# A graph layer on one core: the columns that VectorE and ScalarE pick are shared out anew

## The chip, the cores and the metric

The kernel runs on one core of one Trainium2 chip. The metric is the device time of one launch in microseconds, the median of several runs. The engines are TensorE (PE: matrix multiplies into PSUM), VectorE (DVE), ScalarE (ACT), GpSimd (POOL, which here issues indirect gathers) and SyncE (SP, which here issues other transfers).

## The reference

A message-passing layer over 412,500 edges between 12,500 nodes of 128 features, with a residual and a layer norm. The edges are sorted by their target node. Cut to what matters:

```
f0, f1 = x0 @ W1_0e, x1 @ W1_1o              # first half "feat", second half "self"
e0, e1 = feat0[src], feat1[src]              # a row of 128 per edge, gathered by its source
h  = gelu(gelu(edge_scalar @ W_mlp1) @ W_mlp2)
w00, w01, w10, w11 = h @ Wp_00, h @ Wp_01, h @ Wp_10, h @ Wp_11
mid0 = [w00*e0*ea0, w11*sum(e1*ea1)]         # products of weights, rows and edge attributes
mid1 = [(w01*e0)*ea1, w10*e1*ea0]
n0, n1 = segment_sum(mid0, dst), segment_sum(mid1, dst)
y  = cos*self + sin*(n @ W2)
out = layernorm(x + y)
```

## The kernel before

**Runs and chunks.** 512 edges are a run (`s`), four tiles of 128 edges (`q` = 0 to 3). Four runs are a chunk (`c`), and `k = s % 4` is a run's place in it. There are 806 runs. One loop over `s` writes out, by hand, the order of the instructions on TensorE, ScalarE, VectorE and SyncE; POOL's gathers run as buffers come free, up to 18 runs ahead (`LEAD = 19` buffers `G`).

**Start.** x is loaded, turned (`xT` keeps all of x in SBUF, features on partitions, one column per node), multiplied by the folded weights `wf`, and stored to a table in HBM.

**How a tile of rows gets into `G[s]`.** There are four ways.
- POOL gathers 128 rows of the table by an indirect transfer (line 210). This is the rule.
- In the first 18 runs it gathers rows of x instead. `turn_rows(s)` turns them (TensorE, then a copy by ScalarE), `features(s)` multiplies them by `wf` (TensorE, then a copy by ScalarE, line 569).
- In every 14th run from 36 on, SyncE fetches tile 3 row by row (`aid`, line 197): 16 rows at a time, 6 to 16 runs ahead.
- Tile 2 of some runs is picked by VectorE, and tile 1 of some by ScalarE. The engine loads the byte addresses of the sources' columns from a row in SBUF into its registers (`pick_nodes`, line 167), and copies each column of `xT` (128 partitions, one element each) into a tile `GT` (`pick`, lines 178 and 180). When 128 columns are there, `picked_rows` multiplies the tile by `wf` (TensorE, line 186) and ScalarE copies the result into `G` (line 187), two runs before its use.

`COLS = {DVE: 4, ACT: 5}` says that VectorE takes four runs for a tile and ScalarE five. VectorE loads two times 16 addresses a run, and copies 8 columns after its second multiply and 24 after its third. ScalarE loads 24 or 28 addresses a run. `COL_TURN` fixes at which `k` a finished tile is turned into rows: 0 for VectorE's tiles, 1 for ScalarE's.

**A run's work.** TensorE makes the weights (`weights`, line 550). VectorE multiplies weights and rows into `M` in three parts (`messages`: part 0 at line 592, parts 1 and 2 at line 596). TensorE sums `M` over the edges of each target with selection matrices (`segments`, lines 621 and 623), one run later. Each chunk, VectorE adds the sums to an accumulator (`add`, line 636), with a register load of up to four addresses at every fourth chunk (line 631), and makes the next selection (`select`, lines 577 and 585). For a later chunk ScalarE and TensorE compute the radial network (`radial`, `mlp1`, `mlp2`), all of whose PSUM tiles come from the two buffers called "h", as those of `picked_rows` and `moments` do.

**Norm.** When 512 nodes are complete (about every eighth chunk), `norm` at `k == 3` calls `moments`: TensorE multiplies (lines 653 and 656), ScalarE copies the result to `y` (line 661), VectorE takes mean and variance from PSUM (lines 665 and 666). At every second group `normalise` follows: VectorE, the square root on ScalarE (line 674), VectorE's reciprocal (line 675), scaling by ScalarE (line 688) and the store by SyncE (line 247).

At the loop's second run `addresses` scales the source numbers in SBUF into byte addresses (lines 152 and 154). `aid_load` brings them from HBM beforehand (lines 135 and 143).

Of the kernel before, what the change touches and what calls it, by code (L numbers as in the profile page):

```python
# [8 lines left out]
F32 = mybir.dt.float32  # L9
# [12 lines left out]
P = 128  # L22
# [25 lines left out]
AID_FROM = 36  # L48
AID_LEAD = 16
STEPS = 12  # L50
COLS = {DVE: 4, ACT: 5}
COL_Q = {DVE: Q - 2, ACT: Q - 3}
COL_TURN = {DVE: (8, 0), ACT: (16, 1)}
LNB = 2


# [1 line left out]
def gnn_kernel(ctx: ExitStack, tc: tile.TileContext, x, src, dst, ea4, ea8, w1_0, w1_1, wm1, wm2,  # L58
# [26 lines left out]
    def sub(ap, offset, dims):  # L85
        return bass.AP(tensor=ap.tensor, offset=ap.offset + offset, ap=dims)
# [24 lines left out]
    G, GT, Y = {}, {}, {}  # L111
    aided = range(AID_FROM, NS - 1, AID)

    picked = {}
    for e, per in COLS.items():
        picked[e], (t, k) = [], COL_TURN[e]
        while True:
            at = t + per + 1
            at += (k - at) % CH
            if at + 2 >= NS - 1:  # L120
                break
            picked[e].append((t, at, at + 2))
            t += per
    pick_of = {(e, s): i for e, g in picked.items() for i, (_, _, s) in enumerate(g)}
    assert AID_FROM >= raw_runs and AID_LEAD < LEAD and P % ROWS == 0 and STEPS <= AID
    assert all(raw_runs <= g[0][2] and 0 < len(g) <= 2 * P for g in picked.values())
    assert 0 < len(aided) <= P

    aid_at = cst.tile([len(aided), P], I32)
# [2 lines left out]
    def aid_load():  # L132


        nc.sync.dma_start(aid_at, sub(src, AID_FROM * SB + (Q - 1) * P, [[AID * SB, len(aided)], [1, P]]))
        for e, g in picked.items():
            cycle = CH // math.gcd(CH, COLS[e])
            for h in range(0, len(g), P):
                part = g[h:h + P]
                rows = cst.tile([len(part), P], I32, name=f"pick{len(pick_rows)}")  # L140
                for i in range(min(cycle, len(part))):
                    n = len(part[i::cycle])
                    nc.sync.dma_start(rows[i::cycle], sub(src, part[i][2] * SB + COL_Q[e] * P,
                                                          [[cycle * COLS[e] * SB, n], [1, P]]))
# [10 lines left out]

    picking = {e: [] for e in picked}

    def pick_nodes(e, s, part=0, parts=1):

        per = COLS[e]  # L160
        i, t = divmod(s - COL_TURN[e][0], per)
        if not 0 <= i < len(picked[e]):
            return
        if t == 0 and part == 0:
            GT[e, i] = wk.tile([P, P], F32, name=f"gt{list(picked).index(e)}", bufs=3)
        r0, r1 = (n * (P // 4) // (per * parts) * 4 for n in (t * parts + part, t * parts + part + 1))
        _, r = nc.values_load_multi_w_load_instructions(  # L167
            pick_rows[e, i][:, r0:r1], engines=[e], min_val=x_at, max_val=x_at + 4 * (N - 1),
            skip_runtime_bounds_check_because="addresses of columns")
        for k in range(r1 - r0):  # L170
            at = r[k].with_bounds(guaranteed_mod_val=0, out_of_modulus=4)
            picking[e].append((GT[e, i][:, r0 + k:r0 + k + 1], x_bytes[:, bass.ds(at, 4)].bitcast(F32)))

    def pick(e, n):

# [7 lines left out]
    def picked_rows(e, i):  # L183

        pt = ps.tile([P, P], F32, name="h")
        nc.tensor.matmul(pt, GT.pop((e, i)), wf, start=True, stop=True)  # L186
        nc.scalar.activation(G[picked[e][i][2]][:, COL_Q[e], :], pt, AF.Copy)  # L187

    def aid(s, t):

# [211 lines left out]
    def new_sums():  # L402
        A["next"] = wk.tile([P, 4, ACC], F32, name="acc")
# [237 lines left out]
    def moments(b, sums=None):  # L641
        n0, nn, full, tail, tiles = group(b)
        if not pend:
            Y["y"] = wk.tile([P, LNB, XB, P], F32, name="y", bufs=1)
            Y["v"] = wk.tile([P, LNB * XB, 2], F32, name="mv")
            nc.vector.memset(Y["v"], 1.0)
        j = len(pend)
        pend.append(b)
        pt = ps.tile([P, XB, P], F32, name="h")
        st = wk.tile([P, XB, 6], F32, name="bst")  # L650
        at = n0 - base[-1] if b in due[NCH - 1] else 0
        for t, k in tiles:
            nc.tensor.matmul(pt[:k, t, :], xT[:, n0 + t * P:n0 + t * P + k], ws, start=True, stop=sums is not None)
            if sums is None:
                for a in range(4):
                    nc.tensor.matmul(pt[:k, t, :], A["now"][:, a, at + t * P:at + t * P + k], wpost[:, a, :],  # L656
                                     start=False, stop=a == 3)
            else:
                nc.vector.tensor_tensor(pt[:k, t, :], pt[:k, t, :], sums[:k, t, :], op=OP.add)
        if full:  # L660
            nc.scalar.activation(Y["y"][:, j, :full, :], pt[:, :full, :], AF.Copy)  # L661
        if tail:
            nc.scalar.activation(Y["y"][:tail, j, full, :], pt[:tail, full, :], AF.Copy)
        for t, k in tiles:
            nc.vector.bn_stats(st[:k, t, :], pt[:k, t, :])  # L665
            nc.vector.bn_aggr(Y["v"][:k, j * XB + t, :], st[:k, t, :])

    def normalise(last=False):
        y, mv = Y["y"], Y["v"]
        n = len(pend) * XB  # L670
        a = wk.tile([P, 4, LNB * XB], F32, name="rs")
        v, r, u, m = a[:, 0, :n], a[:, 1, :n], a[:, 2, :n], a[:, 3, :n]
        nc.vector.tensor_scalar(v, mv[:, :n, 1], EPS, None, op0=OP.add)
        nc.scalar.activation(u, v, AF.Sqrt)
        nc.vector.reciprocal(r, u)

        nc.vector.tensor_tensor(u, r, r, op=OP.mult)
        nc.vector.scalar_tensor_tensor(u, v, -0.5, u, op0=OP.mult, op1=OP.mult)
        nc.vector.scalar_tensor_tensor(r, u, 1.5, r, op0=OP.add, op1=OP.mult)
        nc.vector.scalar_tensor_tensor(m, mv[:, :n, 0], -1.0, r, op0=OP.mult, op1=OP.mult)  # L680
        for j, b in enumerate(pend):
            for t, k in group(b)[4]:
                i = j * XB + t
                if last and t % 2:
                    nc.vector.tensor_scalar(y[:k, j, t, :], y[:k, j, t, :], r[:k, i:i + 1], m[:k, i:i + 1],
                                            op0=OP.mult, op1=OP.add)
                    continue
                nc.scalar.activation(y[:k, j, t, :], y[:k, j, t, :], AF.Identity,
                                     bias=m[:k, i:i + 1], scale=r[:k, i:i + 1])
            store_nodes(nc.sync, out, b, y[:, j])  # L690
        pend.clear()

    def norm(bs, last=False):
        for b in bs:
            moments(b)
            if not last:
                move_sums()
                new_sums()
            if len(pend) == LNB or b == 0:
                normalise(last)  # L700
        if last and pend:
            normalise(last)

    odd_f = cst.tile([1, 1], F32)
    odd_i = cst.tile([1, 1], I32)
# [9 lines left out]
    def general():  # L715
# [96 lines left out]
                                         out_offset=bass.IndirectOffsetOnAxis(ap=to, axis=0))  # L812
        for b in range(NG):
            moments(b, load_nodes(b, sums))
            if len(pend) == LNB:
                normalise()
        if pend:
# [2 lines left out]
    with tc.manual_schedule(engines={PE, ACT, DVE, SP}):  # L820
# [41 lines left out]
            mlp2(1)  # L862
        weights(0, range(Q))
        select(0)
        turn_rows(0)
        features(0)
        A["now"] = A["next"]
        clearing = []
        pick_nodes(ACT, 0)
        for s in range(NCH * CH + CH):  # L870
            c, k = divmod(s, CH)
            if s + LEAD - 1 < NS:
# [37 lines left out]
            pick_nodes(ACT, s + 1)  # L910
            if s + 1 < raw_runs:
                turn_rows(s + 1)
            if s < NS:
                messages(s, 0)
                messages(s, 1)
                pick_nodes(DVE, s, 0, 2)
                pick(DVE, P // 16)
                messages(s, 2)
                pick_nodes(DVE, s, 1, 2)
                pick(DVE, P)  # L920
            if s + 1 < raw_runs:
                features(s + 1)
# [47 lines left out]
```

## Time and profile before

| | |
|---|---|
| Median of 3 runs | 3773.7 us (3766.81 to 3779.11) |
| Profiled execution | 3772.84 us, span 3771.0 us |
| Mean granted TensorE clock | 0.914 |
| PE busy | 3274.6 us (87%) |
| DVE busy | 3106.1 us (82%) |
| POOL busy | 2682.6 us (71%) |
| ACT busy | 2594.3 us (69%) |
| Transfers | 240.07 MB, mean 64 GB/s |

The span runs from the first to the last instruction of one profiled execution. Busy time counts an engine's instructions on data. Register loads, semaphores and the issuing of transfers are not in it. "Idle before" a group of instructions is the time in which the engine did nothing just ahead of them; behind the arrow stands what ended it, and "issue" where the profile shows no other engine or transfer. A name such as DVEq is the instruction queue of that engine.

### The profile page before, as it was taken

What the parts mean: (1) busy time and instruction counts of PE and PEld (TensorE: products, weight loads), DVE (VectorE), ACT (ScalarE), POOL (GpSimd) and SP (SyncE); (2) the same over time, 40 slices, a digit from 0 to 9 for tenths busy, and PEclk for the clock granted to TensorE, in tenths of its full rate; (3) what the DMA queues carried; (4) which work ended last, traced back from release to release, by engine and by line L of the source; (5) the groups of instructions that cost most, each with busy time, mean ns of one, the idle gap of its engine ahead of it and who ended that gap; (6) DMA issues with size and microseconds to landing.
All of it is one profiled execution on the core that took longest, in us unless ns stands there. A gap on an engine that the chain in (4) does not pass through costs nothing.

```text
span 3771.0 us, 139554 instructions
## 1 busy us (share of the span) xinstructions
PE 3274.6 (87%) x28566; PEld 2859.2 (76%) x28566; DVE 3106.1 (82%) x28801; ACT 2594.3 (69%) x21604; POOL 2682.6 (71%) x2821
## 2 busy tenths in 40 slices
PE   5888898888898889888889898898898888888998
PEld 4677777777777778777778777777787777777877
DVE  3488888888888888888888888888888888888886
ACT  2367677777767767767777677776776677767774
POOL 7567777777777777777777777777777777767770
PEclk8999898998988999899998899999899999989889
DMA  8222222323222223222223222222322222222220
GB/s 203 47 51 67 61 56 65 64 57 70 61 58 64 63 57 68 64 55 62 62 63 67 61 63 61 61 62 61 68 62 59 59 64 61 60 63 63 58 61 15
DMA packets 579462, 240.07 MB, mean 64 GB/s; under 512 B 483793, under 2 KB 528744, under 8 KB 578616
## 3 DMA queue, kind: packets, MB, share of 16 engines
q0 software_dynamic: 90080, 184.66, 19.1%
q1 hardware_dynamic: 467766, 39.95, 8.7%
q10 hardware_dynamic: 20770, 6.47, 0.7%
q8 instruction: 252, 4.13, 0.5%
q14 instruction: 594, 4.87, 0.4%
HBM read 218.04 MB, written 12.80 MB: 61 GB/s over the span
## 4 chain that ended last, share of the span: by engine, by line
DVE 51%; issue 12%; PE 10%; SPq 9%; DVEq 6%; ACT 5%; DMA 4%; POOL 2%; ACTq 0%; POOLq 0%
DVE gt L178 29%; DVE M L596 14%; SPq L197 7%; DVEq L167 6%; DVE M L592 3%; ACT gt L180 3%; PE sums L621 2%; POOL G L210 2%; PE sums L623 2%; SPq L193 2%; PE h L656 2%; DMA G<-table,idx 1%; DVE acc L636 1%; PE w L550 1%; PE h L517 1%
## 5 line engine op out<-in xcount | busy, mean ns | idle before, releaser
L210 POOL DMA_INDIRECT G<-table,idx x2743 | 2613.7, 953 | 981.2 <-issue 758.4
L180 ACT ACTIVATE gt<-xT 128x1 f32 x19968 | 1953.4, 189 | 255.9 <-issue 254.2
L178 DVE COPY gt<-xT 128x1 f32 x25216 | 1680.1, 144 | 374.2 <-issue 362.4
L623 PE MATMUL sums<-own,M 128*128 128x96 f32 x6446 | 1342.7, 292 | 63.2 <-DVE M L596 62.7
L621 PE MATMUL sums<-own,M 128*128 128x96 f32 x6446 | 1374.7, 297 | 25.0 <-DVE M L596 24.8
L621 PEld LDWEIGHTS sums<-own,M 128*128 128x128 f32 x6446 | 1063.9, 205 | 115.4 <-DVE M L596 31.1
L623 PEld LDWEIGHTS sums<-own,M 128*128 128x128 f32 x6446 | 1061.4, 207 | 84.1 <-DVE M L596 83.2
L550 PE MATMUL w<-wpb,h 64*128 64x128 f32 x6448 | 726.8, 310 | 255.8 <-DVE M L596 254.9
L550 PEld LDWEIGHTS w<-wpb,h 64*128 64x128 f32 x6448 | 540.4, 200 | 426.8 <-DVE M L596 305.8
L596 DVE TENSOR_TENSOR M<-w,G 128x384 f32<-128x384 f32 x1576 | 861.2, 547 | 0.1
L521 ACT ACTIVATE h<-h 128x512 f32<-128x512 f32 x404 | 216.2, 585 | 225.0 <-PE h L517 219.2
L592 DVE TENSOR_TENSOR M<-w,G 128x256 f32<-128x256 f32 x788 | 321.6, 408 | 3.6 <-ACT G L187 2.0
L517 PE MATMUL h<-eT,w1b 64*128 64x128 f32 x3232 | 299.9, 339 | 4.2 <-ACT eT L510 4.2
L517 PEld LDWEIGHTS h<-eT,w1b 64*128 64x128 f32 x3232 | 255.8, 237 | 29.6 <-issue 12.5
L187 ACT ACTIVATE G<-h 128x128 f32<-128x128 f32 x353 | 96.2, 272 | 261.1 <-PE h L186 218.1
L532 PE MATMUL h<-h,w2b 64*64 64x256 f32 x3232 | 236.5, 392 | 7.4 <-ACT h L521 6.3
L537 ACT ACTIVATE h<-h 128x512 f32<-128x512 f32 x404 | 213.6, 578 | 25.1 <-PE h L532 20.0
L532 PEld LDWEIGHTS h<-h,w2b 64*64 64x64 f32 x3232 | 111.1, 133 | 60.5 <-ACT h L521 16.1
L186 PE MATMUL h<-wf,gt 128*128 128x128 f32 x706 | 145.7, 289 | 4.1 <-ACT eT L510 4.1
L585 DVE TENSOR_TENSOR own<-oh,e 128x512 f32<-128x512 f32 x202 | 139.7, 692 | 7.1
L665 DVE BATCH_NORM_STATS2 bst<-h 128x6 f32<-128x128 f32 x98 | 26.9, 274 | 131.2 <-ACT y L661 123.0
L510 ACT ACTIVATE eT<-h 128x128 f32<-128x128 f32 x202 | 53.8, 267 | 111.1 <-PE h L508 105.2
(112 smaller groups left out, 1364.5 us busy)
## 6 DMA issues: line engine op xcount, KB each, us to landing
G<-table SPq DMA_DIRECT2D x7040, 0.5 KB
G<-table,idx POOLq DMA_INDIRECT x2743
e<-in_edge_attr SPq DMA_DIRECT2D x201, 64.0 KB
xt<-in_x SPq DMA_DIRECT2D x24, 256.0 KB
table<-ft ACTq DMA_DIRECT2D x24, 256.0 KB
xt<-in_edge_attr SPq DMA_DIRECT2D x24, 256.0 KB
out<-y SPq DMA_DIRECT2D x24, 256.0 KB
xt<-in_dst SPq DMA_DIRECT2D x5, 256.0 KB
```

What stands on the lines that cost most here:

```text
L167: _, r = nc.values_load_multi_w_load_instructions(pick_rows[e, i][:, r0:r1], engines=[e], min_val=x_at, max_val=x_at + 4 * (N - 1), skip_r ...
L178: nc.vector.tensor_copy(to, col)
L180: nc.scalar.activation(to, col, AF.Copy)
L197: nc.sync.dma_start(G[s][r0 + k:r0 + k + 1, Q - 1, :].bitcast(U8), table_bytes[bass.ds(r[k], P * 4)].rearrange("(a k) -> a k", a=1))
L210: nc.gpsimd.indirect_dma_start(out=G[s][:, q, :], out_offset=None, in_=x if s < raw_runs else table, in_offset=bass.IndirectOffsetOnAxis(a ...
L517: nc.tensor.matmul(p1[h][:, j // 2, j % 2, :], w1b[rows, j, :], eT[c][rows, :], start=True, stop=True)
L532: nc.tensor.matmul(p2[r][k * HID:(k + 1) * HID, h * n:(h + 1) * n], w2b[rows, :], H1[c][h][rows, k * n:(k + 1) * n], start=True, stop=True)
L550: nc.tensor.matmul(WP[i][:, q, :], H2[c][q % 2][rows, k, q // 2, :], wpb[rows, :], start=True, stop=True)
L592: nc.vector.tensor_tensor(M[s][:, :, :, :MUL], w[:, :, :2 * MUL].rearrange("p q (a u) -> p q a u", a=2), g[:, :, None, :MUL].to_broadcast( ...
L596: nc.vector.tensor_tensor(M[s][:, :, j, MUL:].rearrange("p q (i u) -> p q i u", i=3), w[:, :, None, (2 + j) * MUL:(3 + j) * MUL].to_broadc ...
L621: nc.tensor.matmul(flat[:, bass.ds(at, 4 * FIRST_HALF)].bitcast(F32), M[s][:, q, 0, :], own[:, 3 * WIDE:], start=False, stop=False)
L623: nc.tensor.matmul(sb[:, 1:, bass.ds(at, 4 * WIDE)].bitcast(F32), M[s][:, q, 1, :], own[:, :3 * WIDE].rearrange("p (a j) -> p a j", a=3), ...
```

## The change

- VectorE picks 36 columns a run instead of 32, ScalarE 28 instead of about 25.6. VectorE loads 8, 12 and 16 addresses, each followed by as many copies, after its first, second and third multiply. Columns are counted through, so that a tile may end within a group; the load is then split in two. Over the whole run VectorE fills 222 tiles instead of 197, ScalarE 171 instead of 156, and POOL issues 2703 gathers from the table instead of 2743.
- A picked tile is turned into rows two runs after its last column, at whatever `k` that falls.
- The addresses come by 32 transfers instead of 10.
- `statistics` is split from `moments`. It reads `y` in SBUF instead of PSUM, and it and `normalise` come one run later, at `k == 0`, behind that run's multiplies and copies; in the last chunk they follow at once.
- `turn_rows` and `features` run two runs ahead instead of one; those of the first two runs stand ahead of the loop.

```
-COLS = {DVE: 4, ACT: 5}
+SLOTS = {DVE: [(8, 12, 16)], ACT: [(28,)]}
-COL_TURN = {DVE: (8, 0), ACT: (16, 1)}
+COL_FROM = {DVE: 11, ACT: 16}
...
+    slot_at = {}
+    for e, cycle in SLOTS.items():
+        slot_at[e], n = {}, 0
+        for s in range(COL_FROM[e], NS):
+            for slot, k in enumerate(cycle[(s - COL_FROM[e]) % len(cycle)]):
+                slot_at[e][s, slot] = (n, n + k)
+                n += k
...
+            last = P * (len(picked[e]) + 1)
+            at = next((s for (s, _), (_, z) in slot_at[e].items() if z >= last), NS) + 2
             if at + 2 >= NS - 1:
                 break
-            picked[e].append((t, at, at + 2))
+            picked[e].append(at + 2)
...
+    def pick_nodes(e, s, slot):
+        a, z = slot_at[e].get((s, slot), (0, 0))
+        z = min(z, P * len(picked[e]))
+        while a < z:
+            i, r0 = divmod(a, P)
+            r1 = min(P, r0 + z - a)
+            if r0 == 0:
+                GT[e, i] = wk.tile([P, P], F32, name=f"gt{list(picked).index(e)}", bufs=3)
+            _, r = nc.values_load_multi_w_load_instructions(
+                pick_rows[e, i][:, r0:r1], engines=[e], ...)
...
+            a += r1 - r0
...
-        for t, k in tiles:
-            nc.vector.bn_stats(st[:k, t, :], pt[:k, t, :])
+
+    def statistics(b):
+        j = pend.index(b)
+        st = wk.tile([P, XB, 6], F32, name="bst")
+        for t, k in group(b)[4]:
+            nc.vector.bn_stats(st[:k, t, :], Y["y"][:k, j, t, :])
             nc.vector.bn_aggr(Y["v"][:k, j * XB + t, :], st[:k, t, :])
...
-        turn_rows(0)
-        features(0)
+        for s in range(min(2, raw_runs)):
+            turn_rows(s)
+            features(s)
...
-            if s + 1 < raw_runs:
-                turn_rows(s + 1)
+            if s + 2 < raw_runs:
+                turn_rows(s + 2)
             if s < NS:
-                messages(s, 0)
-                messages(s, 1)
-                pick_nodes(DVE, s, 0, 2)
-                pick(DVE, P // 16)
-                messages(s, 2)
-                pick_nodes(DVE, s, 1, 2)
-                pick(DVE, P)
-            if s + 1 < raw_runs:
-                features(s + 1)
+                for part in range(3):
+                    messages(s, part)
+                    pick_nodes(DVE, s, part)
+                    pick(DVE, P)
+            if s + 2 < raw_runs:
+                features(s + 2)
...
-            if k == (1 if end else 3) and 0 < c <= NCH:
-                norm(due.get(c - 1, []), last=c == NCH)
+            if k == 0 and c > 1:
+                norm_on(due.get(c - 2, []))
+            if c == NCH and k == 1:
+                norm_last(due[c - 1])
+            if k == (1 if end else 3) and 0 < c < NCH:
+                norm(due.get(c - 1, []))
```

More of the change, by code (lines that the diff above doesn't have):

```diff
@@ L112, in gnn_kernel @@
     aided = range(AID_FROM, NS - 1, AID)
+    slot_at = {}
[5 more added lines that the diff above has]
+                n += k
     picked = {}
-    for e, per in COLS.items():
-        picked[e], (t, k) = [], COL_TURN[e]
+    for e in SLOTS:
+        picked[e] = []
         while True:
-            at = t + per + 1
-            at += (k - at) % CH
+            last = P * (len(picked[e]) + 1)
+            at = next((s for (s, _), (_, z) in slot_at[e].items() if z >= last), NS) + 2
             if at + 2 >= NS - 1:
                 break
-            picked[e].append((t, at, at + 2))
-            t += per
-    pick_of = {(e, s): i for e, g in picked.items() for i, (_, _, s) in enumerate(g)}
+            picked[e].append(at + 2)
+    pick_of = {(e, s): i for e, g in picked.items() for i, s in enumerate(g)}
     assert AID_FROM >= raw_runs and AID_LEAD < LEAD and P % ROWS == 0 and STEPS <= AID
-    assert all(raw_runs <= g[0][2] and 0 < len(g) <= 2 * P for g in picked.values())
+    assert all(raw_runs <= g[0] and 0 < len(g) <= 3 * P for g in picked.values())
     assert 0 < len(aided) <= P
@@ L136, in aid_load @@
         for e, g in picked.items():
-            cycle = CH // math.gcd(CH, COLS[e])
+            n = sum(sum(run) for run in SLOTS[e])
+            cycle, ahead = n // math.gcd(n, P), P // math.gcd(n, P) * len(SLOTS[e])
+            assert all(z - a == ahead for a, z in zip(g, g[cycle:]))
             for h in range(0, len(g), P):
@@ L141, in aid_load @@
                 for i in range(min(cycle, len(part))):
-                    n = len(part[i::cycle])
-                    nc.sync.dma_start(rows[i::cycle], sub(src, part[i][2] * SB + COL_Q[e] * P,
-                                                          [[cycle * COLS[e] * SB, n], [1, P]]))
+                    k = len(part[i::cycle])
+                    nc.sync.dma_start(rows[i::cycle], sub(src, part[i] * SB + COL_Q[e] * P,
+                                                          [[ahead * SB, k], [1, P]]))
                 pick_tiles.append(rows)
@@ L156, in gnn_kernel @@
     picking = {e: [] for e in picked}
[L158 to L172, printed above, removed]
+    def pick_nodes(e, s, slot):
[7 more added lines that the diff above has]
+            _, r = nc.values_load_multi_w_load_instructions(
+                pick_rows[e, i][:, r0:r1], engines=[e], min_val=x_at, max_val=x_at + 4 * (N - 1),
+                skip_runtime_bounds_check_because="addresses of columns")
+            for k in range(r1 - r0):
+                at = r[k].with_bounds(guaranteed_mod_val=0, out_of_modulus=4)
+                picking[e].append((GT[e, i][:, r0 + k:r0 + k + 1], x_bytes[:, bass.ds(at, 4)].bitcast(F32)))
+            a += r1 - r0
     def pick(e, n):
@@ L186, in picked_rows @@
         nc.tensor.matmul(pt, GT.pop((e, i)), wf, start=True, stop=True)
-        nc.scalar.activation(G[picked[e][i][2]][:, COL_Q[e], :], pt, AF.Copy)
+        nc.scalar.activation(G[picked[e][i]][:, COL_Q[e], :], pt, AF.Copy)
     def aid(s, t):
@@ L649, in moments @@
         pt = ps.tile([P, XB, P], F32, name="h")
-        st = wk.tile([P, XB, 6], F32, name="bst")
         at = n0 - base[-1] if b in due[NCH - 1] else 0
@@ L691, in normalise, with norm, norm_on, norm_last @@
         pend.clear()
-    def norm(bs, last=False):
+    def norm(bs):
         for b in bs:
             moments(b)
-            if not last:
-                move_sums()
-                new_sums()
-            if len(pend) == LNB or b == 0:
-                normalise(last)
-        if last and pend:
-            normalise(last)
+            move_sums()
+            new_sums()
+    def norm_on(bs):
+        for b in bs:
+            statistics(b)
+            if len(pend) == LNB or b == 0:
+                normalise()
+    def norm_last(bs):
+        for b in bs:
+            moments(b)
+            statistics(b)
+            if len(pend) == LNB:
+                normalise(True)
+        if pend:
+            normalise(True)
     odd_f = cst.tile([1, 1], F32)
@@ L814, in general @@
             moments(b, load_nodes(b, sums))
+            statistics(b)
             if len(pend) == LNB:
@@ L864, in gnn_kernel @@
         select(0)
-        turn_rows(0)
-        features(0)
+        for s in range(min(2, raw_runs)):
+            turn_rows(s)
+            features(s)
         A["now"] = A["next"]
         clearing = []
-        pick_nodes(ACT, 0)
+        pick_nodes(ACT, 0, 0)
         for s in range(NCH * CH + CH):
@@ L909, in gnn_kernel @@
             pick(ACT, P)
-            pick_nodes(ACT, s + 1)
-            if s + 1 < raw_runs:
-                turn_rows(s + 1)
+            pick_nodes(ACT, s + 1, 0)
+            if s + 2 < raw_runs:
+                turn_rows(s + 2)
             if s < NS:
-                messages(s, 0)
-                messages(s, 1)
-                pick_nodes(DVE, s, 0, 2)
-                pick(DVE, P // 16)
-                messages(s, 2)
-                pick_nodes(DVE, s, 1, 2)
-                pick(DVE, P)
-            if s + 1 < raw_runs:
-                features(s + 1)
+                for part in range(3):
[4 more added lines that the diff above has]
+                features(s + 2)
             if k == (1 if end else 2) and 0 < c <= NCH:
                 add(c - 1)
-            if k == (1 if end else 3) and 0 < c <= NCH:
-                norm(due.get(c - 1, []), last=c == NCH)
+            if k == 0 and c > 1:
[4 more added lines that the diff above has]
+                norm(due.get(c - 1, []))
                 clearing += [(c, a) for a in range(4)] if c - 1 in due and c < NCH else []
```

## The prediction, made before the changed kernel was run

> **What bounds the kernel now.** I read the busy times and the whole-core groups first, then the stretch of steady work, then the waits, then single instructions. One step of the main loop is one run of 512 edges. The engines' busy times, and the groups of VectorE (DVE), of the gathering engine (POOL) and of ScalarE (ACT), each with count | busy us, mean ns | idle before it:
>
> ```profile
> span 3771.0 us, 139554 instructions
> ...
> PE 3274.6 (87%) x28566; PEld 2859.2 (76%) x28566; DVE 3106.1 (82%) x28801; ACT 2594.3 (69%) x21604; POOL 2682.6 (71%) x2821
> ...
> L178 DVE COPY gt<-xT 128x1 f32 x25216 | 1680.1, 144 | 374.2 <-issue 362.4
> L592 DVE TENSOR_TENSOR M<-w,G 128x256 f32<-128x256 f32 x788 | 321.6, 408 | 3.6 <-ACT G L187 2.0
> L665 DVE BATCH_NORM_STATS2 bst<-h 128x6 f32<-128x128 f32 x98 | 26.9, 274 | 131.2 <-ACT y L661 123.0
> L210 POOL DMA_INDIRECT G<-table,idx x2743 | 2613.7, 953 | 981.2 <-issue 758.4
> L180 ACT ACTIVATE gt<-xT 128x1 f32 x19968 | 1953.4, 189 | 255.9 <-issue 254.2
> ```
>
> The steady stretch from 500 to 3500 us, with each engine's busy time, and VectorE's idle time within the same stretch by what ended it:
>
> ```profile
> core 0: us, PE busy (x) PEld busy (x) DVE busy (x) ACT busy (x) POOL busy (x), PEclk, DMA share, GB/s
> 500.00:3500.00 3000.00, 2635.40 (x23124) 2301.98 (x23124) 2557.87 (x24145) 2159.79 (x18336) 2206.11 (x2315) 0.92 0.29 62
> DVE gt L178 <- issue: 305.1, 765, 1.3
> DVE bst L665 <- ACT y L661: 92.6, 19, 7.5
> ```
>
> VectorE looks only 85% busy (2557.87 of 3000). But 305.1 us more are idle before the column copies of line 178 with no partner to wait for ("issue"), and 92.6 us before the statistics. Together that is 2955.6 us of 3000, 98.5%. It almost never waits for data: the multiplies of line 592, which need both TensorE's weights and the gathered rows, have 3.6 us of idle in the whole run. VectorE is the bound, and its "issue" idle belongs to its own instruction stream.
>
> What that idle is: before each group of column copies the addresses are loaded into registers. The two kinds of register loads on VectorE's queue, then one step of VectorE, then the chain of waits over the same stretch:
>
> ```profile
> L167 DVEq TENSOR_LOAD <-pick x1576: 1093/1122/1740, 149.6 to 3716.9; - x197
> L631 DVEq TENSOR_LOAD <-first_at x51: 342/348/766, 135.8 to 3751.0; - x51
> 2024.96 0.42 DVE L592 TENSOR_TENSOR M<-w,G 128x256 f32<-128x256 f32 x1
> 2025.29 0.55 DVE L596 TENSOR_TENSOR M<-w,G 128x384 f32<-128x384 f32 x1
> 2025.81 0.58 DVE L178 COPY gt<-xT 128x1 f32 x8
> 2026.30 0.55 DVE L596 TENSOR_TENSOR M<-w,G 128x384 f32<-128x384 f32 x1
> 2027.27 1.54 DVE L178 COPY gt<-xT 128x1 f32 x24 [0.42 <-issue]
> 2028.73 0.41 DVE L592 TENSOR_TENSOR M<-w,G 128x256 f32<-128x256 f32 x1
> ...
> 2026.20 0.06 DVEq L167
> 2026.26 0.12 DVE gt L178 x2
> 2026.38 0.47 DVE M L596
> 2026.85 0.42 issue
> ```
>
> A load of 16 addresses takes 1122 ns, one of 4 (line 631 loads four at once) 348 ns: (1122 − 348)/12 = 64.5 ns an address and 90 ns fixed. So 8 cost 0.61 us and 12 cost 0.86 us (estimates from these two rows). A copy costs 61 ns (24 of them between 2027.27 and 2028.73), so **the load of an address costs as much as the copy it serves**. It is free only as far as VectorE still has issued work to run. Here it has not: the second load begins at about 2026.17 (1.10 us ahead of the copies at 2027.27; the chain turns to it at 2026.20). The work issued before it ends at 2026.76: the multiply from 2026.30 with 0.46, what such a multiply holds the engine when work follows it at once (the chain has 0.47). Cover 0.59 us, uncovered 0.51. The first load, behind 24 copies and two multiplies, leaves 0.06 (2025.29 + 0.46 to 2025.81). Uncovered now: 0.57 us a step.
>
> Second in line is POOL. Its gathers follow one another every 1.25 us:
>
> ```profile
> 2027.42 0.94 POOL L210 DMA_INDIRECT G<-table,idx  x1 [0.31 <-issue]
> 2028.66 0.94 POOL L210 DMA_INDIRECT G<-table,idx  x1 [0.30 <-issue]
> POOL G L210 <- DVE M L596: 134.8, 129, 9.9
> POOL G L210 <- PE h L559: 31.1, 16, 3.5
> ```
>
> 2743 × 1.25 = 3429 us: nearly full as well. But it is POOL that waits 134.8 us for VectorE to free row buffers, and not the reverse.
>
> **The change, part by part.** All is set against the profiled execution: 3772.84 us, span 3771.0, 0.9 us under the median of 3773.7. A measurement of this kernel tells about 0.3% (11 us) from no change.
>
> *More columns on VectorE.* The new order of instructions has 222 tiles of 128 columns where there were 197: 25 × 128 = 3200 copies more, at 61 ns = **+195 us**, all on the bound. Nothing hides them.
>
> *Three groups in place of two.* A step becomes: 256-wide multiply, load 8, copy 8; 384-wide multiply, load 12, copy 12; 384-wide multiply, load 16, copy 16. It has 790 such steps. Uncovered load time by the step shown above: instructions are issued every 0.04 us (9 in the 0.36 from 2025.81 to 2026.17). The 12-load stands where the second load stood, behind 8 copies and a multiply: 1.10 − 4 × 0.0645 = 0.84 less cover 0.59 = 0.25. The 16-load starts 13 × 0.04 = 0.52 after the first of 12 copies that last 0.73; cover 0.73 − 0.52 + 0.46 = 0.67, uncovered 0.43. The 8-load (0.58) stands behind 16 copies and the 256-wide multiply (0.33, 2024.96 to 2025.29): 17 × 0.04 = 0.68 of 0.97, cover 0.62, nothing uncovered; I keep 0.06, since the first load of today shows that much. Together 0.74 against 0.57: 0.17 × 790 = **+134 us**. Bounds: all covered, −0.57 × 790 = −450; only the one multiply covers, 0.25 + 0.38 + 0.64 = 1.27, +553. I take the value by the quoted step, as the same engine, instructions and loads are in it.
>
> *Tiles that end within a group.* 128 is no multiple of the groups, so 146 loads are split: 146 × 0.09 = **+13 us** (0 if covered).
>
> *Statistics a step later.* Now VectorE, right after TensorE's products for 512 nodes have been asked for, waits for ScalarE's copy out of them, 131.2 us in all; 128 of it lie before the last group, 23 waits of 5.3 us on average. Afterwards a whole step of VectorE's own work (4.5 us: 3000 us hold 666 steps by the 256-wide multiplies) comes first, and the input is the copy in SBUF. Left over: 23 × 0.8 = 18. What is late next is the square root:
>
> ```profile
> L592 DVE TENSOR_TENSOR M<-w,G 128x256 f32<-128x256 f32 x666 | 271.8, 408 | 1.2 <-DMA G<-table 0.2 <-PE h L186 0.2 <-PE h L508 0.2
> DVE rs L675 <- ACT rs L674: 6.6, 13, 0.6
> SPq L247 <- ACT y L688: 217.7, 23, 21.4
> ACT G L187 <- PE h L186: 218.1, 122, 3.1
> ```
>
> The reciprocal waits 0.5 us for it today, because ScalarE has then just written y and stands idle; a step later ScalarE may have 14 columns ahead of it (14 × 0.098 = 1.4 us, 12 times; +17 at most of this kind, +64 if the whole 5.3 us came back). I take +5. Sum 128 − 18 − 5 = **−105 us** (bounds −128 and −46). The output stores move with it on SyncE's queue, where they already hold 217.7 us; behind them stand the single-row transfers of the fourth tile, issued six steps or more ahead (over 27 us). Cost 0; if that cover were gone, up to one 21.4 us stall each.
>
> *Input-gathered rows two steps ahead.*
>
> ```profile
> DVE M L592 <- ACT ft L569: 57.3, 18, 14.3
> 100.00:130.00 30.00, 24.79 (x209) 21.10 (x209) 11.70 (x55) 8.80 (x17) 19.03 (x21) 0.94 0.17 43
> L143 SPq DMA_DIRECT2D pick<-in_src x10: 309/592/787, 82.4 to 88.4; - x10
> 107.98 0.24 DVE L152 TENSOR_SCALAR aid_at<-aid_at 55x128 int32<-55x128 int32 x1
> ```
>
> In the first 18 steps VectorE waits 57.3 us for ScalarE's rows; the first 14.3 comes ahead of the loop and stays. Of the other 43 TensorE, busy 24.79 of 30 us there, can give back no more than its idle sixth of some 110 us: **−20 us** (bounds 0 and −43). SyncE must issue 32 address transfers instead of 10 (22 × 0.59 = 13 us) before VectorE scales them in the loop's second step; today they are out at 89 and wanted at 108. Cost 0, at most +13.
>
> *ScalarE* gets 171 − 156 = 15 tiles more, 1920 copies × 0.098 = 188 us, hidden in its 1177 us of idle time; *POOL* loses 40 gathers, −50 us, off the bound. Cost 0 both. If ScalarE's cover were gone, 188.
>
> Sum: 195 + 134 + 13 − 105 − 20 = +217; 3772.8 + 217 = **3990 us**.
>
> **The rivals.** *Loads hidden (faster).* If the issuing runs ahead so fast that a load begins with its group's predecessor, cover is the whole predecessor and the next multiply: 0.95 for the 12-load, 1.19 for the 16-load, and nothing stays uncovered. VectorE would then need 3772.8 + 195 − 450 + 13 − 105 − 20 = 3406, and POOL ends last: 3771 − 134.8 − 31.1 − 50 = 3555, some 3600 with its own late starts. It decides as soon as the uncovered time falls under 0.57 − (195 + 13 − 125)/790 = 0.46 us a step. Against it: today's second load has the same predecessor as the new 12-load and is not hidden. [...]
>
> *Loads no worse than now.* The three gaps together stay at 0.57 us: 195 + 13 − 105 − 20 = +83, 3856 us. For it speaks only that the loads are smaller; the longest, 16, keeps its length.
>
> *ScalarE's and TensorE's turn-taking.* Picked tiles are now turned to rows at any step of a chunk, also where the radial network needs the same two PSUM buffers. If half of 393 tiles made TensorE wait 1.8 us (218.1/122 is what ScalarE waits for such a tile), 353 us would join TensorE's 3274.6 busy and 496 idle: 4124 at worst. It decides from 122 tiles on (219 us); against it: TensorE has that idle time and gets more as VectorE slows.
>
> That the change does not do what it says is not open: the order of instructions has the 3200 copies and the 40 gathers fewer.
>
> **How the numbers follow.** The forecast gets 0.76, equal loads 0.10, turn-taking 0.05, hidden loads 0.09. The range goes from the equal loads, 3850, to the forecast with 0.12 us a step more uncovered (95 us), 4085. Faster than the bound 0.09, within it 0.02, slower 0.89.
>
> **What would show it.** Right: VectorE's column copies 28416, their idle time from 374 to about 500 to 560 us with idle before groups of 12 and of 16; the statistics' wait from 131 to some 20; POOL's wait for VectorE up to several hundred us; 4.8 us a step. Wrong: idle before the column copies under 300 us, POOL without waits, or TensorE and ScalarE waiting for each other at line 186's tiles while VectorE waits at its multiplies.

## The result, and the profile after

The changed kernel took 4117.8 us (median of 4 runs, 4108.6 to 4120.5) against 3774.7 before: ratio 1.090, 95% interval 1.088 to 1.092. The profiled execution of it has a span of 4106.9 us, 335.9 more than before. The direction was forecast, the size was not: 343 us more instead of 217, 33 us above the range.

The page of the changed kernel, the rows that answer to those of before (a line number is higher by 10 here for the copies, multiplies and gathers, by 9 for the register loads, by 13 for the norm):

```profile
span 4106.9 us, 146137 instructions
...
PE 3487.0 (85%) x28646; PEld 3049.0 (74%) x28646; DVE 3372.2 (82%) x32001; ACT 2784.2 (68%) x23564; POOL 2651.6 (65%) x2781
...
L220 POOL DMA_INDIRECT G<-table,idx x2703 | 2582.9, 956 | 1338.3 <-issue 954.1
L190 ACT ACTIVATE gt<-xT 128x1 f32 x21888 | 2139.3, 189 | 317.6 <-issue 310.9
L188 DVE COPY gt<-xT 128x1 f32 x28416 | 1949.7, 144 | 483.1 <-issue 458.4
L602 DVE TENSOR_TENSOR M<-w,G 128x256 f32<-128x256 f32 x788 | 321.8, 408 | 4.2 <-ACT G L197 1.5
```

Its groups on VectorE that belong to the norm, and then, of its waits, the one of POOL for VectorE:

```profile
L678 DVE BATCH_NORM_STATS2 bst<-y 128x6 f32<-128x128 f32 x98 | 26.3, 268 | 46.5 <-ACT y L670 45.7 <-issue 0.7
L688 DVE RECIPROCAL rs<-rs 128x8 f32<-128x8 f32 (+1 forms) x13 | 2.6, 201 | 45.4 <-ACT rs L687 45.4
```

```profile
POOL G L220 <- DVE M L606: 135.4, 128, 9.4
```

The steady stretch, VectorE's longest waits in it, and one of its steps on VectorE:

```profile
500.00:3500.00 3000.00, 2571.00 (x21169) 2247.55 (x21171) 2532.81 (x24438) 2114.60 (x18222) 1985.78 (x2080) 0.87 0.26 56
DVE gt L188 <- issue: 350.8, 1185, 0.9
DVE rs L688 <- ACT rs L687: 36.4, 9, 4.5
DVE bst L678 <- ACT y L670: 35.3, 15, 4.8
```

```profile
2038.78 1.06 DVE L188 COPY gt<-xT 128x1 f32 x16 [0.30 <-issue]
2039.76 0.41 DVE L602 TENSOR_TENSOR M<-w,G 128x256 f32<-128x256 f32 x1
2040.17 0.58 DVE L188 COPY gt<-xT 128x1 f32 x8
2040.66 0.55 DVE L606 TENSOR_TENSOR M<-w,G 128x384 f32<-128x384 f32 x1
2041.38 0.82 DVE L188 COPY gt<-xT 128x1 f32 x12 [0.17 <-issue]
2042.12 0.55 DVE L606 TENSOR_TENSOR M<-w,G 128x384 f32<-128x384 f32 x1
```

VectorE is busy 2532.81 us of 3000. With the idle time before copies and in the norm (350.8, 36.4 and 35.3) it is 2955.3, as full as before (2955.6). The step has the forecast parts: 8 copies with nothing idle ahead of them, 12 with 0.17 us, 16 (those of the step before stand first) with 0.30. The idle time before the copies, 483.1, stays under the 500 to 560 us that I had named. POOL's wait for VectorE did not grow to several hundred us either; POOL is idle for longer before its gathers (1338.3, before 981.2), but the page puts that down to "issue" (954.1, before 758.4) and to short waits for several engines.

The 335.9 us come out of these rows. VectorE is busy 3372.2 − 3106.1 = 266.1 us longer: 3200 copies at 61 ns are 195. The other 71 are for the most part ends of multiplies: a wide multiply lasts 0.55 us, and in these traces an instruction that was ready started 0.46 after its start at the earliest. Behind the third group's load nothing is ready then, so 0.09 us a step more count as busy (0.09 × 790 = 71, an estimate); they belong to the uncovered time. The idle time before copies grew by 483.1 − 374.2 = 108.9. The norm's two waits shrank by 131.2 + 6.6 − 46.5 − 45.4 = 45.9. What is left, 6.8, lies in the rest.

### The profile page after: what moved, and what is told of

Read it like the earlier page. It is cut to its first block, busy times and chain, and to the rows that moved or that the text cites. A ratio compares the mean times of both kernels' runs of the same rounds, so it can differ in the third digit from the quotient of the medians.

```text
span 4106.9 us, 146137 instructions
## 1 busy us (share of the span) xinstructions
PE 3487.0 (85%) x28646; PEld 3049.0 (74%) x28646; DVE 3372.2 (82%) x32001; ACT 2784.2 (68%) x23564; POOL 2651.6 (65%) x2781
## 5 line engine op out<-in xcount | busy, mean ns | idle before, releaser
L220 POOL DMA_INDIRECT G<-table,idx x2703 | 2582.9, 956 | 1338.3 <-issue 954.1
L190 ACT ACTIVATE gt<-xT 128x1 f32 x21888 | 2139.3, 189 | 317.6 <-issue 310.9
L188 DVE COPY gt<-xT 128x1 f32 x28416 | 1949.7, 144 | 483.1 <-issue 458.4
L633 PE MATMUL sums<-own,M 128*128 128x96 f32 x6446 | 1386.7, 301 | 73.1 <-DVE M L606 72.4
L631 PE MATMUL sums<-own,M 128*128 128x96 f32 x6446 | 1424.4, 306 | 1.3 <-DVE M L606 0.7
L631 PEld LDWEIGHTS sums<-own,M 128*128 128x128 f32 x6446 | 1111.9, 214 | 95.1 <-issue 27.2
L633 PEld LDWEIGHTS sums<-own,M 128*128 128x128 f32 x6446 | 1106.1, 215 | 91.0 <-DVE M L606 89.7
L560 PE MATMUL w<-wpb,h 64*128 64x128 f32 x6448 | 759.4, 320 | 364.7 <-DVE M L606 364.2
L560 PEld LDWEIGHTS w<-wpb,h 64*128 64x128 f32 x6448 | 579.3, 211 | 530.3 <-DVE M L606 406.2
L527 PE MATMUL h<-eT,w1b 64*128 64x128 f32 x3232 | 365.6, 368 | 38.9 <-ACT G L197 31.8
L527 PEld LDWEIGHTS h<-eT,w1b 64*128 64x128 f32 x3232 | 311.4, 262 | 76.7 <-ACT G L197 37.0
L196 PEld LDWEIGHTS h<-wf,gt 128*128 128x128 f32 x786 | 132.3, 213 | 4.8 <-ACT h L531 4.4
```

Of the source, the lines that this page charges most:

```text
L188: nc.vector.tensor_copy(to, col)
L190: nc.scalar.activation(to, col, AF.Copy)
L220: nc.gpsimd.indirect_dma_start(out=G[s][:, q, :], out_offset=None, in_=x if s < raw_runs else table, in_offset=bass.IndirectOffsetOnAxis(a ...
L527: nc.tensor.matmul(p1[h][:, j // 2, j % 2, :], w1b[rows, j, :], eT[c][rows, :], start=True, stop=True)
L560: nc.tensor.matmul(WP[i][:, q, :], H2[c][q % 2][rows, k, q // 2, :], wpb[rows, :], start=True, stop=True)
L631: nc.tensor.matmul(flat[:, bass.ds(at, 4 * FIRST_HALF)].bitcast(F32), M[s][:, q, 0, :], own[:, 3 * WIDE:], start=False, stop=False)
```

## The experiments

My theory is that VectorE sets the time, and that its step is made of copies, multiplies and the part of each register load that no issued work covers ("cover"); the norm's waits were mostly moved, not removed. The rivals: only the number of columns counts; or TensorE is made late, by a lower granted clock (0.872 against 0.914 over the run) and by picked tiles turned wherever they end. The kernels ran on several chips, on which the kernel before took 3775 to 3781 us; a difference of under some 10 us between two of them tells nothing.

**Groups and columns.** Three kernels differ from the changed one in one line:

```
 changed    SLOTS = {DVE: [(8, 12, 16)], ACT: [(28,)]}
 g36_two    SLOTS = {DVE: [(0, 20, 16)], ACT: [(28,)]}
 g32_three  SLOTS = {DVE: [(8, 8, 16)], ACT: [(28,)]}
 g32_two    SLOTS = {DVE: [(0, 16, 16)], ACT: [(28,)]}
```

> The changed kernel with VectorE's 36 columns a run in two groups (20 after the second multiply, 16 after the third) instead of three; all else as changed. Cover theory (VectorE sets the time; its step is copies at 61 ns, multiplies, and what of each register load is not covered by work issued ahead of it): the load of 20 (90 + 20 x 64.5 ns = 1.38 us) stands behind 16 copies and two multiplies and leaves 0.35 to 0.43 us uncovered, the load of 16 behind 20 copies and one multiply 0.28; together 0.63 to 0.71 against 0.79 measured in the changed kernel, so 60 to 125 us less: 3995 to 4060. Column theory (only the number of columns counts): 4118, no change. TensorE theory (the lower granted clock, 0.872 against 0.914, and picked tiles turned at any step of a chunk make TensorE late): 4118, no change, clock as low as there.

> The changed kernel with 32 columns a run in three groups of 8, 8 and 16; all else as changed. Cover theory: four copies fewer a step (193 us in 790 steps), and uncovered 0.09 (8 behind 16 copies and the first multiply), 0.03 (8 behind 8 copies and a multiply) and 0.50 (16 behind 8 copies and a multiply), 0.62 against 0.79 in the changed kernel, 130 us: about 3800. Column theory: 4118 - 193 = 3925. TensorE theory: 4100 or more.

> The changed kernel with 32 columns a run in two groups of 16 after the second and third multiply; all else as changed. Cover theory: 193 us of copies fewer; uncovered 0.10 to 0.17 (16 behind 16 copies and two multiplies) and 0.37 (16 behind 16 copies and one), 0.47 to 0.54 against 0.79, 200 to 250 us: 3675 to 3725, below the kernel before, unless POOL's gathers, which then have less than 100 us of slack, hold it a little higher. Column theory: 3925. TensorE theory: 4100 or more.

Measured: 4037, 3811 and 3699 us (ratios to before 1.070, 1.008 and 0.979, the last with the interval 0.978 to 0.981). The copies' group in each, in this order:

```profile
L188 DVE COPY gt<-xT 128x1 f32 x28416 | 1877.7, 144 | 415.6 <-issue 337.0
```

```profile
L188 DVE COPY gt<-xT 128x1 f32 x25216 | 1751.9, 144 | 402.5 <-issue 383.8
```

```profile
L188 DVE COPY gt<-xT 128x1 f32 x25216 | 1682.4, 144 | 271.3 <-issue 231.1
```

The uncovered time of a step, that of split loads included, can be taken from all steps between 500 and 3500 us: the start of a group's first copy, less the start of the multiply ahead of it, less the 0.46 us (0.33 for the narrow one) that this multiply holds the engine (two wide ones in a row last 1.01 us in one_group, 0.46 and 0.55). Means, in us:

| kernel | forecast or expected | measured, group by group | sum |
|---|---|---|---|
| before | 0.57 | 0.11, 0.48 | 0.59 |
| changed | 0.74 | 0.09, 0.25, 0.44 | 0.79 |
| g36_two | 0.63 to 0.71 | 0.41, 0.26 | 0.67 |
| g32_three | 0.62 | 0.10, 0.02, 0.51 | 0.62 |
| g32_two | 0.47 to 0.54 | 0.17, 0.30 | 0.47 |

All three times fell where the cover theory put them (3811 against "about 3800"), and the column theory missed by 81, 114 and 226 us. Between the changed kernel and g32_three lie 307 us: four columns a step are 193 of them by the copies' price, 0.17 us less uncovered some 134, and the norm's two waits are 29 us longer there (120.8 against 91.9). Where the loads stand is seen alone in g32_two against g32_three, with the same columns: 112 us, and 0.15 us less uncovered in 790 steps are 119. A third group costs by its load, which finds less cover; behind a group's last copy nothing is lost, the next instruction follows it after 0.06 us.

The TensorE theory misses as well. Tiles are turned wherever they end in all three kernels, yet the clock was 0.881, 0.909 and 0.929 in them: it rises as the time falls. And in the changed kernel VectorE's narrow multiplies, which need TensorE's weights, wait 4.2 us in all from run 18 on.

**How far ahead work is issued.** One group of 32: `SLOTS = {DVE: [(0, 0, 32)], ACT: [(28,)]}`.

> The changed kernel with 32 columns a run in one group after the third multiply. Issued every 0.04 us without a limit, the work ahead covers 1.70 of the 2.15 us load, 0.45 stays uncovered against 0.475 with two groups: about 3680. [...]

Measured: 3753 us; the register loads, and part of one step on VectorE:

```profile
L176 DVEq TENSOR_LOAD <-pick x788: 2096/2154/2932, 163.9 to 3718.3; - x197
```

```profile
2005.13 1.01 DVE L606 TENSOR_TENSOR M<-w,G 128x384 f32<-128x384 f32 x2
2006.67 2.04 DVE L188 COPY gt<-xT 128x1 f32 x32 [0.52 <-issue]
```

The load takes 2154 ns, exactly 90 + 32 × 64.5, so the price per address holds from 4 to 32. Uncovered: 0.64 us on average, not 0.45, so that the work ahead covers 1.51 us and not 1.70. For the smaller groups the cover fits the pace of issue that I read from one step (0.67, 0.62 and 0.47 us uncovered in the table, each as expected by it); what holds it back here is not shown. The time is 3753, some 73 us above the expected 3680: of the 132 us more than g32_two that 0.167 us in 790 steps make, the spans of the two profiled executions show 78 (the medians 54). 28 of the difference are shorter waits in the norm (94 against 122 us), and 12 are fewer pauses inside the groups of copies (10 against 22 us in all); for the rest I have no account.

**The norm alone.** The kernel before with `statistics` split off and `norm_on` a run later, the diff of the change and nothing else.

> The kernel before with one part of the change alone: statistics and normalise one run later, from the copy in SBUF. Moved-wait theory (from the changed kernel's trace: the statistics' wait falls from 131 to 46 us, but the reciprocal's wait for ScalarE's square root rises from 7 to 45): about 46 us saved, 3729, with a wait of 30 to 60 us before the reciprocal. The prediction's reckoning: 105 us saved, 3670. If VectorE were not the bound: 3775.

Measured: 3711 us, 69 less. Its rows:

```profile
L668 DVE BATCH_NORM_STATS2 bst<-y 128x6 f32<-128x128 f32 x98 | 26.2, 267 | 20.8 <-ACT y L660 20.8
L678 DVE RECIPROCAL rs<-rs 128x8 f32<-128x8 f32 (+1 forms) x13 | 2.6, 201 | 38.8 <-ACT rs L677 38.8
```

78 us of waiting went and 69 us of time: what VectorE waits less, the kernel gains, almost one for one. It is between the 46 and the 105 that were expected. The statistics' wait falls to 21 as I had reckoned (18), and the square root's wait, for which I had 12, is 39.

**The norm put back.** The changed kernel with the norm's old code and place.

> The changed kernel with the norm in its old place (statistics from PSUM directly behind TensorE's products, normalise behind them); all else as changed. Moved-wait theory: the part is worth there what its waits differ by, 46 to 69 us: 4164 to 4187. The prediction's reckoning: 105 us, 4223. If the norm's waits were hidden in the changed kernel: 4118.

Measured: 4200 us, 83 more than the changed kernel, between the two expectations (4164 to 4187, and 4223).

```profile
L675 DVE BATCH_NORM_STATS2 bst<-h 128x6 f32<-128x128 f32 x98 | 26.9, 274 | 178.8 <-ACT y L671 175.9 <-ACT y L673 2.9
L685 DVE RECIPROCAL rs<-rs 128x8 f32<-128x8 f32 (+1 forms) x13 | 2.6, 201 | 6.8 <-ACT rs L684 6.8
```

In its old place the statistics' wait would be 178.8 us, 48 more than before the change: the other parts make ScalarE's copy of `y` come later. That copy waits in its turn for TensorE's products (132.8 us in all, 121.3 before the change); which of the parts delays them is open. So the part is worth 94 us of waiting there (178.8 + 6.8 − 46.5 − 45.4), near the forecast's 105, but it starts from a longer wait, of which 92 us stay.

**The square root's wait.** The changed kernel, with `normalise` cut after the square root; the reciprocal and the rest follow at `k == 1`.

```
         nc.scalar.activation(u, v, AF.Sqrt)
-        nc.vector.reciprocal(r, u)
...
+            if k == 1 and Y.pop("due", False):
+                scale()                        # reciprocal and what follows
```

> The changed kernel with the reciprocal, and all that follows it in normalise, one run after ScalarE's square root instead of directly behind it. Moved-wait theory: the wait before the reciprocal falls from 45 to under 10 us and VectorE, the bound, gains as much: 4118 - 40 = 4078. If the wait only moves on (to the scaling by ScalarE, or into the next multiply): 4118.

Measured: 4089 us, 29 less.

```profile
L696 DVE RECIPROCAL rs<-rs 128x8 f32<-128x8 f32 (+1 forms) x13 | 2.5, 192 | 0.3 <-ACT rs L687 0.3
```

The wait is gone (45.4 to 0.3) and two thirds of it came out of the time.

What the wait was made of stands in the traces. ScalarE and VectorE around one square root in the changed kernel, then in the kernel before:

```profile
2290.52 1.39 ACT L190 ACTIVATE gt<-xT 128x1 f32 x14
2291.82 0.26 ACT L520 ACTIVATE eT<-h 128x128 f32<-128x128 f32 x1
2291.97 1.40 ACT L190 ACTIVATE gt<-xT 128x1 f32 x14
2294.29 1.28 ACT L687 ACT_TABLE_LOAD   x1 [0.92 <-issue]
2295.58 0.21 ACT L687 ACTIVATE rs<-rs 128x8 f32<-128x8 f32 x1
2291.43 0.17 DVE L686 TENSOR_SCALAR rs<-mv 128x8 f32<-128x8 f32 x1
2295.82 0.20 DVE L688 RECIPROCAL rs<-rs 128x8 f32<-128x8 f32 x1 [4.21 <-ACT rs L687]
```

```profile
2113.07 1.28 ACT L674 ACT_TABLE_LOAD   x1
2113.89 0.17 DVE L673 TENSOR_SCALAR rs<-mv 128x8 f32<-128x8 f32 x1
2114.61 0.20 DVE L675 RECIPROCAL rs<-rs 128x8 f32<-128x8 f32 x1 [0.55 <-ACT rs L674]
```

The input of the square root is ready at 2291.60. ScalarE then has 18 columns and a copy ahead of it, idles 0.92 us while it loads the next run's addresses into registers, and spends 1.28 us on an ACT_TABLE_LOAD, an instruction of its own that stands under the line of the square root. Before the change the same instruction ran while VectorE was still at its statistics, so that only 0.55 us of waiting were left. Of the 45.4 us, ScalarE spent 19.2 on columns and other copies, 9.0 idle behind its register load, 14.1 on ACT_TABLE_LOAD and 2.7 on the square root.

**Picked tiles at a fixed place.** In the changed kernel, `at += ((0 if e == DVE else 1) - at) % CH` after the line that sets `at`.

> The changed kernel with picked tiles turned to rows at a fixed place of the chunk as before (first run for VectorE's tiles, second for ScalarE's) instead of two runs after the last column wherever that falls. Cover theory: little; only the statistics' wait may fall from 46 us towards the 21 us that it has where the norm alone is changed: 4090 to 4118. TensorE theory (turn-taking at the two PSUM buffers costs what is not explained by the copies and loads, some 100 us): 4000 to 4050.

Measured: 4082 us, 35 less (28 by the spans), a little under the 4090 to 4118 of the cover theory and above the 4000 to 4050 of the TensorE theory; copies and norm of it:

```profile
L189 DVE COPY gt<-xT 128x1 f32 x28288 | 1942.7, 144 | 478.9 <-issue 457.7 <-DMA G<-table 1.2
...
L679 DVE BATCH_NORM_STATS2 bst<-y 128x6 f32<-128x128 f32 x98 | 26.3, 268 | 32.7 <-ACT y L671 32.6
```

One tile fewer fits (128 copies, 8 us), and the statistics' wait loses 14 us. The mean uncovered time is 0.78 us, as in the changed kernel. This line does more than move the place, though. At 36 columns a run VectorE fills a tile every 3.6 runs, and a fixed place comes every fourth run, so that some tiles fall on the same run, where only the later is turned: TensorE multiplies 368 tiles instead of 393, and POOL issues 2728 gathers instead of 2703, while VectorE still picks 221. So turning tiles anywhere costs at most some 25 us here, a part of it by way of `y`; the TensorE theory's 70 to 120 are not there.

**Rows one run ahead.** The changed kernel with `turn_rows` and `features` as before the change.

> The changed kernel with the input-gathered rows turned and multiplied one run ahead as before instead of two. From the traces, in which run 18 starts at 209.7 us before and 207.9 after: 2 us, 4118 to 4122. The prediction's reckoning: 20 us slower, 4138.

Measured: 4126 us, 8 more. VectorE's wait for those rows:

```profile
DVE M L602 <- ACT ft L579: 67.7, 18, 17.0
```

It is 52.3 in the changed kernel, with 7.1 more for TensorE's weights. The 8 us are less than these times can tell for certain. Set against the kernel before, nothing is gained: all idle time before these multiplies was 57.3 us there and is 60.4 in the changed kernel.

**What is left to gain.** g32_two with both norm waits put off (`norm_on` at `k == 1`, `scale` at `k == 2`):

> Two groups of 16 columns as in the run before of that form (3699), with statistics another run later and the reciprocal one run after the square root. Cover theory: of its 73 us before the statistics and 49 us before the reciprocal most go, 3580 by VectorE alone; POOL, whose waits of about 150 us are all that it could give back, then ends nearly as late, so 3590 to 3640. If the waits only move: 3699.

Measured: 3672 us, a miss. Both waits are gone, but a new one stands in their place:

```profile
L416 DVE MEMSET acc<- 128x512 f32 x100 | 48.5, 485 | 99.4 <-ACT acc L419 63.2 <-DMA G<-table,idx 32.2
...
L678 DVE BATCH_NORM_STATS2 bst<-y 128x6 f32<-128x128 f32 x98 | 26.1, 266 | 0.5 <-ACT y L670 0.5
```

VectorE's clearing of the next accumulator, in the first run after the norm's products, waits (63.2 of the 99.4 us by this row) for ScalarE to have moved the sums; with the statistics' wait ahead of it, it had waited 5.5 us (g32_two). The next kernel begins the clearing two runs later, and another also fixes the place where tiles are turned:

```
-                clearing += [(c, a) for a in range(4)] if c - 1 in due and c < NCH else []
+                clearing += [(c, a) for a in (None, None, 0, 1, 2, 3)] if c - 1 in due and c < NCH else []
```

> Two groups of 16, both norm waits put off, the clearing begun two runs later. Moved-wait theory: the 99 us before the clearing go: 3575 by VectorE; POOL ends at 3565 or later, so 3580 to 3640. If the wait moves on once more: 3672.

> The same with picked tiles turned to rows at a fixed place of the chunk as before. Cover theory: 0 to 20 us under the run without it. TensorE theory: 40 us or more under it.

Measured: 3647 and 3617 us (the latter 0.958 of before, 0.955 to 0.960). With the clearing put off its idle time is 5.6 us, but only 25 us came out, less than expected; most of the wait went on, to the statistics (now 16.8 us), the reciprocal (22.5) and the narrow multiplies (35.1, before 9.1):

```profile
L418 DVE MEMSET acc<- 128x512 f32 x100 | 48.5, 485 | 5.6
...
L680 DVE BATCH_NORM_STATS2 bst<-y 128x6 f32<-128x128 f32 x98 | 26.2, 267 | 16.8 <-ACT y L672 16.1 <-issue 0.7
...
L698 DVE RECIPROCAL rs<-rs 128x8 f32<-128x8 f32 (+1 forms) x13 | 2.6, 201 | 22.5 <-ACT rs L689 22.5
```

The fixed place takes 30 us more off, between the 0 to 20 of the one theory and the 40 of the other. With 32 columns no two tiles fall on the same run, and as many tiles are turned as without the fixed place (368): here the place alone is changed. The multiplies' wait falls from 35.1 to 11.9 us, the statistics' from 16.8 to 4.6. POOL's longest waits there, and VectorE's for gathered rows:

```profile
POOL G L221 <- issue: 744.0, 2414, 7.8
POOL G L221 <- DMA G<-table,idx: 37.6, 123, 0.3
POOL G L221 <- DVE M L609: 33.9, 111, 0.3
DVE M L605 <- DMA G<-table,idx: 1.5, 2, 1.3
```

No wait of POOL for VectorE is longer than 0.3 us, the gap between most gathers: POOL gathers there almost without a break (before the 2414 gathers behind "issue" it is idle 0.31 us on average, once 7.8), and its last gather starts at 3555.7 of 3607.5 us. VectorE waits for its rows no more than 1.5 us in all, so it still sets the time, with POOL close behind. That fewer columns on VectorE, and so more gathers on POOL, would now make it slower is likely, but no run shows it.

These last two kernels and the one group of 32 also ran on a chip on which the kernel before took 5514 us; there they took 0.988, 0.979 and 0.999 of that. Groups of copies have pauses of 0.4 to 1.2 us on it (read from the one group of 32 between 3003 and 3021 us; the same kernel on the other chip shows none between 2000 and 2014 us), and nothing here is concluded from it.

## Why the prediction was right, and where it was wrong

**Right: the bound and the mechanism.** VectorE was full before and is full after, the loads' idle time grew although no load got longer, POOL lost 40 gathers and gave nothing for it. g32_two and b_norm show the bound from the other side: what VectorE is relieved of comes out of the time.

**Term by term**, forecast and measured: copies 195 and 195 us. Loads with splits, 147 and 180 (71 + 108.9). Steps without a split load left 0.76 us uncovered, 0.17 more than the 0.59 before, as forecast (131 us against 134). A split load left 0.16 to 0.20 us more than another, not 0.09: 146 of them are some 26 us instead of 13. The other 23 us are not in these means. Norm −105 and −45.9. Rows two ahead −20 and nothing that the balance shows. The rest, 6.8. Sum 217 and 336.

**Wrong: the norm's term,** 59 of the 119 us. Two steps of it failed. The reciprocal's wait was to grow by 5 us, at most by 17 from 14 columns ahead of the square root on ScalarE (1.4 us a time); it grew by 38.8, to 3.5 us a time. The columns and copies ahead were mis-sized in the value taken, but near the 17: they took 19.2 us. What the reckoning put at nothing is ScalarE's ACT_TABLE_LOAD ahead of the square root, 14.1 us, which had run beside VectorE's statistics before, and ScalarE's own register load, 9.0 us. The other step is the statistics' wait, for which 18 us were to be left over; 46.5 are. It was reckoned from the wait of before, while the change's other parts lengthen it by 48 us in its old place (norm_undone); in the new place, turning tiles anywhere is at most 14 us of it (turn_fixed), and what the rest comes from is open. That the bound of −46 was met is luck: it was made of 18 us left over and 64 us of the whole wait coming back, not of these two.

**Wrong: the rows two ahead,** 20 us taken from TensorE's idle share. Run 18 starts at 207.9 us instead of 209.7. No wait went: 60.4 us against 57.3. TensorE is as busy there as before (84.4 of 103 us, before 87.1 of 107), so its idle sixth was not given back; that it could be was never shown by a row, and what holds it is open.

**The rivals.** Hidden loads: ruled out by 0.25 and 0.44 us uncovered at the loads of 12 and 16. Equal loads: ruled out by 0.79 against 0.59. Turn-taking: real but small, 30 us in two_clear_fixed and at most 25 in turn_fixed, instead of 219 and more.

**The range** ended at 4085 since it allowed for uncertainty in the loads alone, above. The norm's own upper bound, 59 us more, would have carried it past the measured time.

## What to carry to other kernels

Idle time with no releaser ahead of operations with run-time addresses was here the load of these addresses into registers. Count it as work of that engine (here 90 ns and 64.5 ns an address, about as much as the 61 ns of the copy it serves), and place it behind the longest work that is already issued. More and smaller pieces cost time here, and so did a single large one: 32 columns a run took 3811 us in three groups, 3699 in two and 3753 in one. Ask also what another engine has to do between the input and the result that is waited for: an instruction that ran unseen beside other work (here 1.28 us ahead of each square root but the last) counts once that work is gone. Moving a wait to a later place is worth what is left after the next wait in the same chain has been found: here the wait went from the statistics to the square root and from there to the clearing of a buffer, and of what was taken away only a part came out: 29 us of 45, 25 of 94.

## What was not expected of the hardware

A register load on VectorE is straight in its length over all that ran: 348 ns for 4 addresses, 1122 for 16, 2154 for 32. Its cover, however, fell short of the pace of issue with many copies ahead: behind 32 copies and three multiplies it is 1.51 us on average (2.15 less the 0.64 uncovered), where issuing every 0.04 us would give 1.70. Why is not shown.
